# Messages of a graph network by seven products, edges later in the block, and an opening in another order

## The chip, the cores and the metric

The kernel runs on one core of a Trainium2 chip, in f32 throughout. The metric is the device time of one execution in microseconds (us); lower is better. Five engines work beside each other, each with its own queue in order: PE (TensorE, with its weight loads shown as PEld), DVE (VectorE), ACT (ScalarE), POOL (GpSimd) and SP (SyncE, which here only issues DMAs; ACT issues some too). They wait for each other by semaphores.

## The reference

The input x is 128 batches of 128 nodes with 256 features, adj is 128 adjacency matrices of 128x128. Two layers, each x + layer(relu(layernorm(x))). With h the normed input, layer 0 computes for each batch:

```
xc    = h transposed (features x nodes)
conv  = bn2(conv1d(relu(bn1(conv1d(xc, conv1_w))), conv2_w, 17 taps, pad 8))
x_conv= relu(conv + xc) transposed back
s     = h @ w_se.T + b_se                      # 3 numbers for each node
dist  = |s_n|^2 + |s_m|^2 - 2 s_n . s_m
A     = exp(-dist) * adj
msg   = relu(h @ w_msg.T + b_msg)
x_nmp = A @ msg
gi    = concat(x_conv, x_nmp) @ w_ih.T + b_ih  # 512 -> 768: r, z, n
gh    = h @ w_hh.T + b_hh                      # 256 -> 768: r, z, n
r, z  = sigmoid(gi_r + gh_r), sigmoid(gi_z + gh_z)
out   = (1 - z) * tanh(gi_n + r * gh_n) + z * h
```

Layer 1 is five small graph convolutions (256 to 512 to 256 features) over five fixed groups of the first 25 nodes of each batch, weighted by a softmax and added.

## The kernel before

Features lie on the partitions, in C = 2 halves of 128; the 128 batches are 32 blocks of BB = 4 (T = 512 columns). The stages follow each other, named here with their times in the profiled execution:

1. 0 to about 170 us, the heads of the first 64 batches (`heads`, L264; `head_stats`, `head_norm`, `head_turn`, `head_conv1`, `head_spectra`, L184 to L249): layer norm on DVE with a power on POOL (L196), transposes on PE (L212), the 1-wide convolution (L226), and the forward Fourier products (L241). In between, written out by hand through `some_spectra` (L364), the spectra of the 17-tap weights are made on PE (L165) in eight chunks; each loads a tile `w2` (L152, two buffers), issued on ACT's queue when the chunk before has ended (L371), and writes its result to `vd` in memory (L175). `constants()` (L119) folds the first batch norm into the weights `wc1` of L226; it runs up to its first `yield` after the first transposes (L385).
2. About 170 to 280 us and 390 to 489 us, `spectral` (L285) for the first and the second 64 batches: products by frequency (L312, L317), with the weights' spectra `v` read from `vd` (L294, three buffers, on SP's queue) and their sums `vs` made on POOL (L309). Between the two, 280 to 390 us, the heads of the second 64 batches. `gate_weights` (L331) makes sums of the gate weights on POOL inside the second spectral stage.
3. 489 to about 1780 us, `gates` for the 32 blocks (L592). The gates are four units (L602): r from three inputs (h, x_conv, x_nmp), the part of n from h, the part of n from the two others, and z from three. Each unit multiplies in quarters by a scheme of seven products in place of eight (L604 to L633), for which the inputs are first turned into sums `t` by `gate_inputs` (L578: x_nmp on DVE, the others on POOL) and the products are combined on ACT, DVE and POOL while they leave the PSUM banks. `bank()` (L92) hands out the eight banks in rotation.
4. Up to 1917.7 us, the rest of layer 1 (L833), which otherwise is woven into stage 3 with `back` (L750).

Around the change: while the units of block i go on, `step()` (L1006) is called after each product, and on every other turn it advances the generator `beside_gates(i + 1)` (L954), which makes what block i + 1 will need: `messages` (L509, two halves), `conv_out` (L490, two halves), `edge_terms` (L532, transposes of the distance terms `lr`), `edges` (L541, the exponentials) and `x_nmp` (L556, two halves), with the parts of `back(i - 1)`, called `ends`, between. What is left is finished in the hook `nxt` (L1021), in the z unit, which then makes the inputs of block i + 1 with `gate_inputs`. In messages, each of the four batches is one bank with two matmuls of 259 columns (256 of the message, 3 of the distance):

```python
nc.tensor.matmul(ps[:, :D + 3], ht[:, c, b * N:(b + 1) * N], wms[:, c, :], start=c == 0, stop=c == C - 1)
nc.vector.tensor_tensor(msg[:, b, :], ps[:, :D], bms[:, :D], op=ALU.add)
nc.vector.tensor_tensor(lr[:, 1, b, 0:3], ps[:, D:D + 3], bms[:, D:], op=ALU.add)
```

In the first block there is no earlier block to work beside: `begin` (L987) runs up to the edges ahead of it, and `sums_ahead` (L993) finishes it inside the first unit.

Of the kernel before, what the change touches and what calls it, by code (L numbers as in the profile page):

```python
# [13 lines left out]
P = 128  # L14
# [12 lines left out]
HID = 512  # L27

# [46 lines left out]
def gnn_kernel(ctx: ExitStack, tc: tile.TileContext, io, out0: bass.AP, out1: bass.AP):  # L75
# [38 lines left out]
    def constant_loads():  # L114
        nc.sync.dma_start(vec, io["vec"])
        nc.sync.dma_start(wc1, io["wc1"].rearrange("(c p) o -> p c o", p=P))
        nc.sync.dma_start(fd, io["fd"])
# [31 lines left out]
    vd = dram.tile([C, D // WCH, P, LW, WCH], F32, tag="vd", name="vd")  # L149
    yd = [dram.tile([HG, 2, LW, D], F32, tag=f"yd{h}", name=f"yd{h}") for h in range(NH)]  # L150

    def taps_load(pool, c, q, queue, split=1):  # L152
        w2 = pool.tile([P, WCH // 4, P], F32, tag="w2", name="w2", bufs=2)
# [4 lines left out]
    def weight_spectra(pool, c, q, w2):  # L158
# [16 lines left out]
        nc.scalar.dma_start(vd[c, q], sp)  # L175
# [109 lines left out]
    def spectral(bp, X, h, amid):  # L285

        for p0 in range(0, NP_, 4):
            amid.get(p0, lambda: None)()
            ys = bp.tile([P, 4, 2, D], F32, tag="ys", name="ys", bufs=2)
            for p in range(p0, p0 + 4):  # L290
                if p % 2 == 0:
                    v = bp.tile([P, C, D // WCH, 4, WCH], F32, tag="v", name="v", bufs=3)
                    for c in range(C):
                        nc.sync.dma_start(v[:, c], vd[c, :, :, 2 * p:2 * p + 4, :].rearrange("q i d o -> i q d o"))  # L294
# [36 lines left out]
    def gate_weights():  # L331
        tt = nc.gpsimd.tensor_tensor
        for k in range(3):
# [9 lines left out]
    with front as es:  # L343
# [7 lines left out]
        with ExitStack() as ws:  # L351
# [7 lines left out]
            nc.scalar.dma_start(gt, io["gt"])  # L359
            taps = [taps_load(wp, *todo[0], nc.sync, split=4)]  # L360
# [3 lines left out]
            def some_spectra(k=1):  # L364
                for _ in range(k):
                    if not spectra and todo:
                        spectra.append(weight_spectra(wp, *todo.pop(0), taps.pop(0)))
                    if spectra and next(spectra[0], STOP) is STOP:
                        spectra.pop(0)
                        if len(todo) > 1:  # L370
                            taps.append(taps_load(wp, *todo[1], nc.scalar))  # L371
# [7 lines left out]
            nc.sync.dma_start(fw, row("fw", 5))  # L379
            head_stats(hk, 0)  # L380
            some_spectra()
            head_norm(0)
            some_spectra()
            head_turn(hk, 0)
            consts = constants()  # L385
            next(consts)
            some_spectra()
# [13 lines left out]
        wms = gw.tile([P, C, D + 3], F32)  # L401
        bms = gw.tile([P, D + 3], F32)
# [4 lines left out]
        def small_loads():  # L407
            nc.sync.dma_start(idm, io["idm"])
            nc.sync.dma_start(wms, io["wms"].rearrange("(c p) o -> p c o", p=P))
            nc.sync.dma_start(bms, row("bms", D + 3))  # L410
# [79 lines left out]
    def conv_out(i):  # L490
# [4 lines left out]
        for o in range(C):  # L495
# [7 lines left out]
            u = wk.tile([P, T], F32, tag="el", name="u", bufs=2)  # L503
            nc.vector.scalar_tensor_tensor(u, ps, sc2[:, o:o + 1], ht[:, o, :], op0=ALU.mult, op1=ALU.add)  # L504
            nc.scalar.activation(xc[:, o, :], u, AF.Relu, bias=sh2[:, o:o + 1])
# [3 lines left out]
    def messages(i):  # L509

        ht = hts[i]
        msg = wk.tile([P, BB, D], F32, tag="msg", name="msg", bufs=1)
        for b in range(BB):
            ps = bank()
            for c in range(C):
# [652 lines left out]
```

## Time and profile before

| | |
|---|---|
| median of 3 runs | 1919.29 us (1916.35 to 1928.1) |
| profiled execution, its own time | 1919.48 us |
| its span, first to last instruction | 1917.7 us |
| granted TensorE clock, mean | 0.995 |
| busy: PE, PEld, DVE, ACT, POOL | 1890.3, 1646.4, 1303.9, 720.5, 609.1 us |
| stage 3 without its begin, 520 to 1780 us: PE, DVE, ACT, POOL busy | 1258.6, 922.4, 492.1, 435.9 us |
| L516 (messages), PE | 512 records of 128x259 |
| L517 and L518, DVE | 128 of 128x256, mean 414 ns; 128 of 128x3, mean 149 ns |
| DMA | 248872 packets, 265.8 MB |

An f32 matmul leaves two records in the profile. Matmuls overlap in the array, so the busy time of one record (385 ns for L516) is longer than the distance from its start to the next start; what a matmul costs is that distance. The chain of waits lists, in order of time, the piece of work that the end depended on at each moment, its start, its length, and how many instructions it holds. The list of waits gives, for one engine and line, what it waited for, the sum, the number of times and the longest.

### The profile page before, as it was taken

To read this page: it belongs to the slowest core of one execution; us is meant where nothing else is said; L and a number is where in the kernel's file an instruction comes from. 1 tells how busy PE (TensorE), PEld (TensorE's weight loads), DVE (VectorE), ACT (ScalarE), POOL (GpSimd) and SP (SyncE) were. 2 spreads that over 40 slices of the span, in tenths; PEclk is the share of its full clock that TensorE was granted. 3 is DMA by queue.
4 is the path that set the end of the run, shared out by engine and by line. 5 is a ranking of instruction groups with operands and counts; after the bars stand their busy time and mean duration, and the time that the engine had idled before them with its cause. 6 is when DMAs were issued, how large, how long until landed. Compare 5 with 4: busy or idle time off the path is not lost.

```text
span 1917.7 us, 30432 instructions
## 1 busy us (share of the span) xinstructions
PE 1890.3 (99%) x10610; PEld 1646.4 (86%) x10610; DVE 1303.9 (68%) x3247; ACT 720.5 (38%) x1555; POOL 609.1 (32%) x678
## 2 busy tenths in 40 slices
PE   8999999999999999999999999999999999999998
PEld 7888889988788888888888888888888888888887
DVE  5676557744677777777666677777756677787643
ACT  4553114411333343343343443333343434334334
POOL 1012531255234334433322233433322233443300
PEclk9999999999999999999999999999999999999999
DMA  8786896379842333333234433233334434222135
GB/s 322 288 312 226 297 311 235 121 241 306 256 117 73 74 95 76 81 90 106 71 94 97 130 97 87 73 82 108 75 90 97 144 72 107 65 78 71 36 92 151
DMA packets 248872, 265.81 MB, mean 139 GB/s; under 512 B 106866, under 2 KB 223943, under 8 KB 244239
## 3 DMA queue, kind: packets, MB, share of 16 engines
q1 hardware_dynamic: 236639, 196.70, 36.9%
q10 hardware_dynamic: 12080, 67.16, 9.0%
q8 instruction: 85, 1.39, 0.3%
q14 instruction: 68, 0.56, 0.1%
HBM read 178.66 MB, written 85.14 MB: 138 GB/s over the span
## 4 chain that ended last, share of the span: by engine, by line
PE 88%; DMA 4%; DVE 4%; issue 2%; ACT 1%; POOL 1%; SPq 0%; ACTq 0%; POOLq 0%; DVEq 0%
PE bank L612 45%; PE bank L317 6%; PE bank L516 5%; PE bank L937 5%; PE bank L877 5%; PE bank L226 4%; PE bank L312 3%; PE bank L563 3%; PE bank L498 3%; PE bank L241 3%; PE bank L165 2%; PE bank L501 1%; PE bank L788 1%; PE bank L856 1%; DMA v<-vd 1%
## 5 line engine op out<-in xcount | busy, mean ns | idle before, releaser
L612 PE MATMUL bank<-t,sw 128*128 128x256 f32 x1152 | 291.6, 380 | 0.7 <-DVE u L504 0.7
L625 POOL TENSOR_TENSOR u<-u,m 128x256 f32<-128x256 f32 x128 | 93.2, 728 | 612.7 <-ACT m L623 545.0
L612 PEld LDWEIGHTS bank<-t,sw 128*128 128x128 f32 x1152 | 215.8, 191 | 31.1 <-issue 2.3
L612 PE MATMUL bank<-t,wih 128*128 128x256 f32 x768 | 197.2, 379 | 0.0
L612 PEld LDWEIGHTS bank<-t,wih 128*128 128x128 f32 x768 | 143.4, 190 | 19.3 <-issue 0.5
L309 POOL TENSOR_TENSOR vs<-v 128x512 f32<-128x512 f32 x78 | 101.3, 1318 | 114.8 <-DMA v<-vd 49.4
L516 PE MATMUL bank<-wms,ht 128*128 128x259 f32 x512 | 124.1, 385 | 0.0
L226 PE MATMUL bank<-wc,ht 128*128 128x256 f32 x512 | 121.4, 391 | 1.6 <-ACT ht L213 1.6
L612 PE MATMUL bank<-xn,wih 128*128 128x256 f32 x384 | 114.9, 381 | 3.6 <-DVE xn L566 3.6
L612 PE MATMUL bank<-t,whh 128*128 128x256 f32 x384 | 115.0, 381 | 0.0
L612 PE MATMUL bank<-xc,wih 128*128 128x256 f32 x384 | 114.8, 381 | 0.0
L937 PE MATMUL bank<-w,hh 128*125 128x256 f32 (+9 forms) x480 | 113.5, 380 | 1.0 <-DVE hh L882 1.0
L226 PEld LDWEIGHTS bank<-wc,ht 128*128 128x128 f32 x512 | 98.0, 196 | 16.7 <-ACT ht L213 3.5
L516 PEld LDWEIGHTS bank<-wms,ht 128*128 128x128 f32 x512 | 98.3, 192 | 15.1
L612 PE MATMUL bank<-ht,whh 128*128 128x256 f32 x384 | 109.9, 380 | 0.0
L877 PE MATMUL bank<-ax,w 128*128 128x500 f32 (+8 forms) x416 | 107.0, 396 | 0.7 <-DMA w<-in_w_dram 0.7
L520 ACT ACTIVATE msg<-msg 128x512 f32<-128x512 f32 x64 | 40.3, 630 | 174.1 <-DVE msg L517 174.1
L630 DVE TENSOR_TENSOR u<-bank,u 128x256 f32<-128x256 f32 x128 | 53.7, 420 | 73.6 <-PE bank L612 73.5
L196 POOL TENSOR_TENSOR rs<-ve,mhalf 128x4 f32<-128x4 f32 x32 | 32.3, 1009 | 217.8 <-DVE ve L194 217.8
L307 DVE SCALAR_TENSOR_TENSOR s<-X 128x256 f32<-128x256 f32 x78 | 47.3, 612 | 79.4 <-PE bank L317 79.1
L937 PEld LDWEIGHTS bank<-w,hh 128*125 128x125 f32 (+9 forms) x480 | 84.3, 177 | 19.2 <-DVE hh L882 1.4
L657 ACT ACTIVATE nn<-nn,vec 128x512 f32<-128x512 f32 x64 | 46.2, 722 | 133.4 <-DVE nn L656 133.4
(187 smaller groups left out, 4279.5 us busy)
## 6 DMA issues: line engine op xcount, KB each, us to landing
v<-vd SPq DMA_DIRECT2D x80, 512.0 KB
vd<-sp ACTq DMA_DIRECT2D x8, 2560.0 KB
yd<-ys ACTq DMA_DIRECT2D x40, 512.0 KB
w<-in_w_dram SPq DMA_DIRECT2D x40, 512.0 KB
htd<-ht ACTq DMA_DIRECT2D x32, 512.0 KB
ht<-htd SPq DMA_DIRECT2D x32, 512.0 KB
ym<-yd SPq DMA_DIRECT2D x32, 512.0 KB
xt<-in_xT_dram SPq DMA_DIRECT2D x32, 512.0 KB
```

The source lines that it names most:

```text
L226: nc.tensor.matmul(pv[:, bb, :], ht[:, c, b * N:(b + 1) * N], wc1[:, c, :], start=c == 0, stop=c == C - 1)
L241: nc.tensor.matmul(ps[:, bb * 2 * LW:(bb + 1) * 2 * LW], h1[:, 2 * h + bb, c * P:(c + 1) * P], fd, start=True, stop=True)
L309: nc.gpsimd.tensor_tensor(vs, vr, vi, op=ALU.add)
L312: nc.tensor.matmul(p1[:, :D], a[:, c], vs[:, c], start=c == 0, stop=c == C - 1)
L317: nc.tensor.matmul(ps[:, k * D:(k + 1) * D], u[:, c], w[:, c], start=c == 0, stop=c == C - 1)
L498: nc.tensor.matmul(ps[:, b * N:(b + 1) * N], ym[:, b, o * P:(o + 1) * P], idm, start=b == 0, stop=False)
L516: nc.tensor.matmul(ps[:, :D + 3], ht[:, c, b * N:(b + 1) * N], wms[:, c, :], start=c == 0, stop=c == C - 1)
L563: nc.tensor.matmul(ps[:, b * N:(b + 1) * N], msg[:, b, c * P:(c + 1) * P], e[:, b, :], start=True, stop=True)
L612: nc.tensor.matmul(ps, w, d, start=n == 0, stop=n == len(pairs) - 1)
L625: nc.gpsimd.tensor_tensor(got["u4"], got["u2"], got["m5"], op=ALU.add)
L877: nc.tensor.matmul(pv[:, q - q0, :], w1s[k5 + g][:, c, q * P:(q + 1) * P], xv[:, c], start=c == 0, stop=c == C - 1)
L937: nc.tensor.matmul(ps[:n1, :D], hh[:, q, at:at + n1], w2s[k5 + g][:, q, :], start=q == 0, stop=q == HID // P - 1)
```

## The change

The messages are made by the same scheme of seven products as the gates: two batches to a product, 130 columns each (256 + 3 padded to 2 x 130), from the weights' quarters and their sums `swm`, which `gate_weights` makes in an additional step on POOL, and from h and its sums t2. The last product (p4) needs t4 of the block, so `gate_inputs(i, (2,))` is called one block ahead, with two buffers. The results are combined by six additions out of PSUM on DVE, one addition in SBUF on DVE, a copy on ACT and two additions on POOL; the distances come out of the message tile by a copy. `edges` goes two turns later, into the unit of n's inputs, and `x_nmp` follows one turn later than before. `conv_out` works in xc itself without a tile u; in block 0 the second half of xn is copied by ACT. In the opening, `vec` is loaded on ACT's queue ahead of the first x, `constants()` runs up to its first yield ahead of the first norm, three steps of the tap spectra in place of two come ahead of the first transposes, and w2 has three buffers, the third filled early by SP. `vd` is laid out by pairs of frequencies, so that a read takes contiguous 4 KB for each partition, and the write goes in pieces of 1 KB. In numbers of instructions, PE goes from 5500 to 5692, DVE 3249 to 3248, ACT 1648 to 1681, POOL 683 to 752.

```diff
@@ -25,6 +25,7 @@
 HID = 512
+MW = 130
@@ -112,7 +113,6 @@
     def constant_loads():
-        nc.sync.dma_start(vec, io["vec"])
         nc.sync.dma_start(wc1, io["wc1"].rearrange("(c p) o -> p c o", p=P))
@@ -146,11 +146,11 @@
     htd = [dram.tile([P, C, T], F32, tag=f"ht{i}", name=f"htd{i}") for i in range(NBLK)]
-    vd = dram.tile([C, D // WCH, P, LW, WCH], F32, tag="vd", name="vd")
+    vd = dram.tile([C, NP_ // 2, P, D // WCH, 4, WCH], F32, tag="vd", name="vd")
     yd = [dram.tile([HG, 2, LW, D], F32, tag=f"yd{h}", name=f"yd{h}") for h in range(NH)]
...
     def taps_load(pool, c, q, queue, split=1):
-        w2 = pool.tile([P, WCH // 4, P], F32, tag="w2", name="w2", bufs=2)
+        w2 = pool.tile([P, WCH // 4, P], F32, tag="w2", name="w2", bufs=3)
         for t in range(0, WCH // 4, WCH // 4 // split):
@@ -172,7 +172,7 @@
             yield
-        nc.scalar.dma_start(vd[c, q], sp)
+        nc.scalar.dma_start(vd[c, :, :, q].rearrange("u i d o -> i u (d o)"), sp.rearrange("p (u d) o -> p u (d o)", d=4))
@@ -291,7 +291,7 @@
                     for c in range(C):
-                        nc.sync.dma_start(v[:, c], vd[c, :, :, 2 * p:2 * p + 4, :].rearrange("q i d o -> i q d o"))
+                        nc.sync.dma_start(v[:, c], vd[c, p // 2])
                 vr, vi = v[:, :, :, 2 * (p % 2), :], v[:, :, :, 2 * (p % 2) + 1, :]
@@ -330,6 +330,15 @@
         tt = nc.gpsimd.tensor_tensor
+
+        a11, a12, a21, a22 = wms[:, 0, 0], wms[:, 1, 0], wms[:, 0, 1], wms[:, 1, 1]
+        s2, s3, s4 = (swm[:, j] for j in range(3))
+        tt(s3, a11, a21, op=ALU.subtract)
+        tt(a21, a21, a22, op=ALU.add)
+        tt(s2, a21, a11, op=ALU.subtract)
+        tt(s4, a12, s2, op=ALU.subtract)
+        tt(bms[:, 1], bms[:, 1], bms[:, 0], op=ALU.subtract)
+        yield
         for k in range(3):
@@ -357,6 +366,7 @@
             nc.scalar.dma_start(gt, io["gt"])
+            nc.scalar.dma_start(vec, io["vec"])
             taps = [taps_load(wp, *todo[0], nc.sync, split=4)]
@@ -367,8 +377,8 @@
                         spectra.pop(0)
-                        if len(todo) > 1:
-                            taps.append(taps_load(wp, *todo[1], nc.scalar))
+                        if len(todo) > 2:
+                            taps.append(taps_load(wp, *todo[2], nc.scalar))
                         some_spectra()
@@ -377,14 +387,15 @@
             nc.sync.dma_start(fw, row("fw", 5))
+            taps.append(taps_load(wp, *todo[2], nc.sync))
             head_stats(hk, 0)
+            consts = constants()
+            next(consts)
             some_spectra()
...
             some_spectra()
+            some_spectra()
             head_turn(hk, 0)
-            consts = constants()
-            next(consts)
-            some_spectra()
             head_stats(hk, 1)
@@ -398,16 +409,17 @@
         idm = gw.tile([P, N], F32)
-        wms = gw.tile([P, C, D + 3], F32)
-        bms = gw.tile([P, D + 3], F32)
+        wms = gw.tile([P, C, 2, MW], F32)
+        bms = gw.tile([P, 2, MW], F32)
+        swm = gw.tile([P, 3, MW], F32)
         wih = gw.tile([P, 2 * C, 3 * D], F32)
...
             nc.sync.dma_start(idm, io["idm"])
-            nc.sync.dma_start(wms, io["wms"].rearrange("(c p) o -> p c o", p=P))
-            nc.sync.dma_start(bms, row("bms", D + 3))
+            nc.sync.dma_start(wms, io["wms"].rearrange("(c p) (q o) -> p c q o", p=P, q=2))
+            nc.sync.dma_start(bms.rearrange("p q o -> p (q o)"), row("bms", 2 * MW))
@@ -500,29 +512,52 @@
                              start=False, stop=True)
-            u = wk.tile([P, T], F32, tag="el", name="u", bufs=2)
-            nc.vector.scalar_tensor_tensor(u, ps, sc2[:, o:o + 1], ht[:, o, :], op0=ALU.mult, op1=ALU.add)
-            nc.scalar.activation(xc[:, o, :], u, AF.Relu, bias=sh2[:, o:o + 1])
+            nc.vector.scalar_tensor_tensor(xc[:, o, :], ps, sc2[:, o:o + 1], ht[:, o, :], op0=ALU.mult, op1=ALU.add)
+            nc.scalar.activation(xc[:, o, :], xc[:, o, :], AF.Relu, bias=sh2[:, o:o + 1])
             yield
...
-        ht = hts[i]
-        msg = wk.tile([P, BB, D], F32, tag="msg", name="msg", bufs=1)
-        for b in range(BB):
-            ps = bank()
-            for c in range(C):
-                nc.tensor.matmul(ps[:, :D + 3], ht[:, c, b * N:(b + 1) * N], wms[:, c, :], start=c == 0, stop=c == C - 1)
-            nc.vector.tensor_tensor(msg[:, b, :], ps[:, :D], bms[:, :D], op=ALU.add)
-            nc.vector.tensor_tensor(lr[:, 1, b, 0:3], ps[:, D:D + 3], bms[:, D:], op=ALU.add)
-            if b % 2:
-                nc.scalar.activation(msg[:, b - 1:b + 1, :], msg[:, b - 1:b + 1, :], AF.Relu)
-                if b == 1:
-                    yield
-        msgs[i] = msg
+
+        msg = wk.tile([P, BB, 2, MW], F32, tag="msg", name="msg", bufs=1)
+        b11, b12, b21, b22 = quarters(hts[i])
+        t1, t2, t3, t4 = (ts[i][2][:, m] for m in range(4))
+        s2, s3, s4 = (swm[:, m] for m in range(3))
+        ops = ((wms[:, 0, 0], b11), (wms[:, 1, 0], b21), (s4, b22), (wms[:, 1, 1], t4), (wms[:, 0, 1], t1), (s2, t2), (s3, t3))
+
+        def product(j):
+            w, d = ops[j - 1]
+            ps = bank()[:, :2 * MW].rearrange("p (b o) -> p b o", b=2)
+            for b in range(2):
+                nc.tensor.matmul(ps[:, b, :], d[:, b * N:(b + 1) * N], w, start=True, stop=True)
+            return ps
+
+        def part(name):
+            return wk.tile([P, 2, MW], F32, tag=name, name=name, bufs=2)
+
+        def biases(q):
+            return bms[:, q, None, :].to_broadcast([P, 2, MW])
+
+        m1, u2, m5, u4, u3 = (part(n) for n in ("m1", "u2", "m5", "u4", "u3"))
+        nc.vector.tensor_tensor(m1, product(1), biases(0), op=ALU.add)
+        nc.vector.tensor_tensor(msg[:, 0:2, 0], product(2), m1, op=ALU.add)
+        nc.vector.tensor_tensor(u2, product(6), m1, op=ALU.add)
+        nc.scalar.copy(m5, product(5))
+        nc.gpsimd.tensor_tensor(u4, u2, m5, op=ALU.add)
+        nc.gpsimd.tensor_tensor(u2, u2, biases(1), op=ALU.add)
+        yield
+        nc.vector.tensor_tensor(msg[:, 2:4, 0], product(3), u4, op=ALU.add)
+        nc.vector.tensor_tensor(u3, product(7), u2, op=ALU.add)
+        nc.vector.tensor_tensor(msg[:, 0:2, 1], u3, product(4), op=ALU.subtract)
+        nc.vector.tensor_tensor(msg[:, 2:4, 1], u3, m5, op=ALU.add)
+        mf = msg.rearrange("p b q o -> p b (q o)")
+        for b in range(0, BB, 2):
+            nc.scalar.activation(mf[:, b:b + 2, :D], mf[:, b:b + 2, :D], AF.Relu)
+        msgs[i] = mf
         sv = lr[:, 1, :, 0:3]
-        nc.vector.tensor_scalar(lr[:, 0, :, 0:3], sv, 2.0, None, op0=ALU.mult)
+        nc.vector.tensor_copy(sv, mf[:, :, D:D + 3])
+        nc.vector.tensor_scalar(lr[:, 0, :, 0:3], mf[:, :, D:D + 3], 2.0, None, op0=ALU.mult)
         s2 = wk.tile([P, BB, 3], F32, tag="sse", name="sse", bufs=2)
@@ -562,7 +597,7 @@
                                  start=True, stop=True)
-            if c:
+            if c and i:
                 nc.vector.tensor_copy(xn[:, c, :], ps)
@@ -581,7 +616,7 @@
             d = d[i]
-            t = wk.tile([P, 4, H], F32, tag=f"t{k}", name=f"t{k}")
+            t = wk.tile([P, 4, H], F32, tag=f"t{k}", name=f"t{k}", bufs=1 + k // 2)
             b11, b12, b21, b22 = quarters(d)
@@ -970,9 +1005,11 @@
                 yield
+            next(ends, None)
+            yield
+            yield
+
             edges(i)
-            yield
-            next(ends, None)
             yield
@@ -984,10 +1021,12 @@
     degs = degrees(*degree_loads())
+    gate_inputs(0, (2,))
     begin = beside_gates(0)
...
         next(begin)
-    gate_inputs(0, (2, 0))
+    gate_inputs(0, (0,))
+    gate_inputs(1, (2,))
     held = [6]
@@ -1022,7 +1061,9 @@
             if i + 1 < NBLK:
-                gate_inputs(i + 1)
+                gate_inputs(i + 1, (0, 1))
+            if i + 2 < NBLK:
+                gate_inputs(i + 2, (2,))
@@ -1103,8 +1144,9 @@
     d.update(_spectral_constants())
-    d["wms"] = cc(np.concatenate([w["w_msg"], w["w_se"]]).T)
-    d["bms"] = cc(np.concatenate([w["b_msg"], w["b_se"]]))
+    pad = np.zeros((2 * MW - w["w_msg"].shape[0] - 3, w["w_msg"].shape[1]), np.float32)
+    d["wms"] = cc(np.concatenate([w["w_msg"], w["w_se"], pad]).T)
+    d["bms"] = cc(np.concatenate([w["b_msg"], w["b_se"], pad[:, 0]]))
     d["wih"] = cc(w["w_ih"].T)
```

## The prediction

> **What bounds the kernel now.** I read the page first, then the spans of the core, the critical chain inside one block of the steady stretch, the waits of PE, the chain over the first 30 us and the groups of instructions.
>
> ```profile
> span 1917.7 us, 30432 instructions
> PE 1890.3 (99%) x10610; PEld 1646.4 (86%) x10610; DVE 1303.9 (68%) x3247; ACT 720.5 (38%) x1555; POOL 609.1 (32%) x678
> ```
>
> PE is the bound from end to end. A busy share of 99% says little by itself, so I asked the chain for one block, 875 to 915 us:
>
> ```profile
> 874.94 4.32 PE bank L612 x20
> 879.26 1.75 PE bank L516 x8
> 881.01 2.59 PE bank L612 x12
> 883.60 1.75 PE bank L516 x8
> ...
> 900.58 0.89 PE bank L563 x8
> 901.48 1.73 PE bank L612 x8
> ```
>
> There is no foreign piece in it: PE issues matmul records back to back, and a block lasts 36.92 us from one L516 to the next. An f32 matmul leaves two records, so 8 message matmuls are 16 records. The spacing follows: 259 columns 1.75/8 = 218 ns, 256 columns (L612) 216 ns, 128 columns (L563) 0.89/8 = 112 ns. Start-to-start differences of the single records give 136 ns for 160 columns (L241) and again 112 ns for 91 and for 48 columns: below about 130 columns something else than the moving columns sets the pace. Only work taken from PE, or waits of PE, can change the time. The waits that the profile names:
>
> ```profile
> PE bank L165 <- DMA gt<-in_gt_dram: 3.9, 1, 3.9
> PE bank L612 <- DVE xn L566: 3.6, 1, 3.6
> PE bank L212 <- issue: 2.6, 1, 2.6
> PE bank L165 <- DMA w<-in_w2t_dram: 2.4, 1, 2.4
> PE bank L241 <- ACT X L249: 2.3, 1, 2.3
> ```
>
> All are singles, in the opening and at the change to the gates (489 to 520 us); the steady blocks have none.
>
> **What the Trainium skill says.** "TensorE: Matmul & The Clock Gate", section Back-to-back issue gap: the spacing is set by weight load and matmul together; section LDWEIGHTS: a load costs its columns over 1.2, about 107 ns for 128, whatever the rows. The trace agrees: 48, 91 and 128 columns all at 112 ns, with 128-column loads. "SBUF — State Buffer", Who interferes with whom: GpSimd shares a port with VectorE's second operand. The trace agrees: the Pool subtraction L588 takes 907 and 1172 ns at 877.7 and 879.4 us, where the same shape alone takes 720. "ScalarE: Activation LUTs", What ACT_TABLE_LOAD costs: about 1283 ns, which is the trace's duration too.
>
> **The change part by part.**
>
> *Messages, PE.* Removed per block: 16 records of 259 columns x 218.5 ns = 3.50 us. Added: seven products of two batches, 14 matmuls, 28 records of 130 columns. No row shows 130. The floor is 112 ns; the line through 160 (136) and 256 (216) gives 136 - 30 x 0.83 = 111, so the bounds are 112 and 116 (a little overhead on the two extra columns). I take 112: 28 x 0.112 = 3.14 us. Gain 0.36 us, x 32 blocks = 11.5; at 116 it is 8. Multiplying less by one eighth gives only a tenth, because short products fall on the weight floor.
>
> *Messages, evictions.* Out: four DVE additions of 128x256 (414 ns) and four of 128x3 (149): 2.25 us. In: six PSUM additions of 128x260 at about 420, one SBUF addition 410, a small copy 150: 3.1 us on DVE; a copy on ACT (0.36); two additions on Pool (0.73 to 1.17 each); ACT's two Relus stay. None is on the path if banks come free in time. Eight banks rotate in order of issue, so the ninth product after p1 (order 1,2,6,5, two products of the gates, 3,7,4) is p4, and it waits for p1's eviction. From the block shown: messages start at 879.10 by single records, p4 is due at 884.37; DVE does its first message eviction at 883.35 (it is still at the state update of the block before), so p1's is done at 883.77: margin about 0.6 us. The next, a gates product that needs p2's bank, has 1.4 us. Pool's last t of this block's input (L589) ends at 882.9 against 884.37. Cost 0, margin thin.
>
> *Edges.* They move two turns later, x_nmp one. From edges to x_nmp's second half: a table load 1.28, four exps, a DVE product, together about 3.3 us against 3.9 of products between. Cost 0, margin 0.6. The transposes of the distances at 891.3 need the lr chain, done about 888.7. Cost 0. Three small lines of DVE go, one copy comes.
>
> *t2 a block ahead.* Pool's order stays t0 then t2, merely for another block; two buffers. 0. The u tile goes (xc in place): 0.
>
> *gate_weights.* Five Pool operations of 128x130 (about 0.4 each, 2 us) in the second spectral stage, where Pool is busy 56.5 of 99 us: 0.
>
> *Third tap buffer.* Before, at 56.2 us the chain turns to the DMA of w2 and PE stands 2.4 to 2.6 us at 67. With the load issued one chunk earlier it has landed. -2.6, between -2.6 and 0: the DMA engines are 75 to 90% busy until 140 us, so a third early load also delays others.
>
> *vd layout.* Reads become 4 KB per packet in place of 1 KB. Packet records: 1 KB 50 ns, 4 KB 160 ns; a v load of 512 KB pays 32 x 50 = 1.6 us per engine before, 8 x 160 = 1.3 after. Stage times at 81 to 87% DMA share thus fall under the load's limit. The stalls that spacing shows at 230 to 252 (L309 on Pool waits 49.4 us for v, mostly covered) and at 467 are together about 3.3; I take -2.5 (-3.3 to -1). The write becomes 1 KB pieces in place of 20 KB: 2.5 MB over 16 engines are 160 x 8 = 1280 packets x 50 ns = 64 us of engine time against 53 (64 x 834 ns). The last write is issued at 139.3 and the first v load follows it; it lands some 1 to 2 us later, and PE's stall of 2.5 us at 153 grows: +1.0 (-0.5 to +2).
>
> *Opening.* The constants' chain goes ahead of the first norm:
>
> ```profile
> 7.74 2.51 issue
> 10.25 2.25 PE bank L212 x8
> 12.50 3.65 PE bank L165 x64
> 16.14 2.00 PE bank L138 x8
> 18.15 1.94 PE bank L165 x32
> 20.09 5.26 PE bank L226 x16
> ```
>
> Nine small DVE operations, two Pool pows (0.7 to 1.0 each, with a hand-over both ways) and a 512-wide copy are about 3.7 us before head_norm(0), so the transposes go from 10.25 to about 14; one more spectra step (32 records, 1.8 us) is pulled into the gap of 2.5 us, which grows. L226, the first thing that depends on both, starts at about 21.5 instead of 20.1. +1.5 (+0.5 to +2.5). vec on ACT's queue, ahead of ln0, delays ln0 by its own issue (an issue on ACT's queue lasts 0.33 to 0.35 in the chain); taken into that range.
>
> *Change to the gates, 489 to 520.* The stall of 3.6 us on xn is set by the chain degrees, edges, x_nmp. i=0's xn copy goes to ACT, behind which DVE's reductions no longer stand; but the DVE list puts the degree reductions, gated by loads landing at 507 to 512, ahead of the first state update, and the first p6 must wait for Pool's t2, some 1.8 us. 0 (-4 to +2). Block 1's stalls at 557 and 560 (0.8 and 1.0): -0.5.
>
> *Sum* on the profiled execution's own 1919.48: -11.4 - 2.6 - 2.5 + 1.0 + 1.5 + 0 - 0.5 = -14.5, so 1905. The median of the runs, 1919.29, is the same to 0.2. The runs spread from 1916.35 to 1928.1; about 1% (19.2 us) is what a measurement of this kernel can tell from no change.
>
> **The rivals.**
>
> *A: as summed*, 1905, own range 1900 to 1911.
>
> *B: PE gains less in the messages.* Spacing 116 to 120, or a wait of 0.2 us in each p4, takes 4 to 7 back: 1909 to 1916, say 1912. For it: no row of 130 columns, and the margin of 0.6. Against: the line through the neighbours ends on the floor.
>
> *C: the early stalls go as well.* The opening costs nothing (1.5), the xn stall (3.6) halves, 557 and 560 and the 1.3 at 38 vanish: 1905 - 1.5 - 2 - 2.5 = 1899, and up to 1896. For it: xn's copy leaves DVE, which was the releaser. Against: the degree loads land when they did.
>
> *D: slower, by DVE's queue.* DVE's fourth message addition needs u4 from Pool, which needs the ACT copy of p5. DVE is in order: behind the addition stand the evictions of the gates' products, and behind these PE's banks. Pool has subtractions of 1.17 us back to back until 882.9. If u4 comes late, DVE stands and PE with it. A delay under 0.6 us is free, each further one counts in full: over 1% slower needs 33.5 us beyond 1905, 1.1 us in each of 31 blocks, so an eviction 1.7 us late. Place: between the second half of the messages and L501; price then about 1942. For it: Pool goes up by two operations in its busiest spot, DVE by 0.85 us. Against: Pool finishes 1.5 us before p4 is due, and DVE has 127 us idle in 442 of the steady stretch (314.7 busy).
>
> *E: the change does nothing visible there*: PE would have to be bound elsewhere. The steady chain has no such piece, so it is contained in B.
>
> **How the numbers follow.** A 0.53, B 0.21, C 0.17, D 0.09. The predicted time is A's, 1905. The range holds A and B and most of C: 1897 to 1916; D and the edge of C are left out. Faster by over 1% (under 1900.1): most of C, a sliver of A: 0.17. Slower by over 1% (over 1938.5): most of D, 0.07. Within 1%: 0.76.
>
> **What would show it.** Messages' row: 28 x 32 = 896 records of 128x130 with 112 ns spacing, a piece of eight lasting 0.89 to 0.90 us; period 36.56 in place of 36.92. No wait of PE on a message addition in the steady blocks; if there is one, D or B. No w2 wait near 67. L226's first start near 21.5. The stall before the first gates still 2 to 4 us. A block period of 36.9 or more makes the prediction wrong in its main term; a period right and a total off by over 5 us makes the opening or the change of stage wrong.

## The result, and the profile after

The changed kernel takes 1943.28 us (median of 4 runs, 1934.57 to 1944.25) against 1918.37 (4 runs); the ratio is 1.0111, 95% interval 1.0077 to 1.0145. It is slower, and outside the forecast's range. The first lines of the page after:

```profile
span 1942.0 us, 31350 instructions
PE 1892.0 (97%) x10994; PEld 1654.5 (85%) x10994; DVE 1320.2 (68%) x3246; ACT 722.3 (37%) x1588; POOL 666.0 (34%) x747
```

PE's busy time is nearly the same as before, though the messages now take less of it, and the span is 24.3 us longer: the time went into gaps, and, as shown below, into matmuls at a lower clock. Where, the moments of the traces tell (us from the span's start; read off the start of the named instruction):

| | before | after | difference |
|---|---|---|---|
| first layer norm (x has landed) | 6.08 | 11.23 | +5.2 |
| first transposes | 10.25 | 18.86 | +8.6 |
| first convolution | 20.02 | 26.77 | +6.8 |
| first spectral product | 173.14 | 197.36 | +24.2 |
| first spectral product, second half | 385.61 | 411.87 | +26.3 |
| transposes of distances, fifth block | 633.22 | 658.23 | +25.0 |
| the same, last block | 1766.64 | 1790.03 | +23.4 |
| end | 1917.69 | 1941.99 | +24.3 |

Nearly all of the loss is there at the first spectral product. Over the 27 blocks that follow the fifth's transposes only 1.6 us come back, where 9.7 were forecast. The waits of PE (sum, times, longest):

```profile
PE bank L165 <- ACT sp L173: 10.2, 5, 3.7
PE bank L212 <- DVE ln L202: 8.4, 1, 8.4
PE bank L165 <- DMA gt<-in_gt_dram: 3.9, 1, 3.9
PE bank L226 <- ACT ht L213: 3.5, 5, 1.1
```

The wait for w2 is gone, as forecast. The first row was one wait of 0.4 us before: PE waits for ACT to copy tap spectra out of PSUM. The chain of the first 200 us shows what ACT did instead:

```profile
1.68 9.53 DMA ln<-in_x_dram
...
18.86 2.10 PE bank L212 x8
...
43.38 0.45 ACTq L175
43.92 5.25 ACTq L155
49.21 0.43 ACT sp L173
49.69 1.99 PE bank L165 x26
51.68 6.56 PE bank L226 x16
...
68.50 3.30 ACTq L155
...
88.94 4.39 ACTq L155
...
103.89 3.67 PE bank L226 x16
...
108.78 3.39 ACTq L155
...
164.50 3.39 ACTq L214
```

ACTq is ACT's queue at a DMA issue. Right after six of the eight writes of vd (L175) the next issue, a tap load (L155) or once a store (L214), holds ACT for 3.3 to 5.3 us; before, the tap loads took 0.37 to 2.00, and this was the longest:

```profile
37.02 2.00 ACTq L155 DMA_DIRECT2D w<-in_w2t_dram  x1
```

Behind a held issue stand the copies (L173) and behind these PE. The same 16 records of L226 take 6.56 us right after such a gap and 3.67 later: the granted clock falls too. By windows (length, busy times of PE, PEld, DVE, ACT and POOL, clock, DMA share, GB/s), after and then before:

```profile
44.00:58.00 14.00, 9.98 (x55) 8.04 (x53) 4.28 (x15) 3.58 (x11) 1.01 (x1) 0.63 0.87 321
```

```profile
44.00:58.00 14.00, 14.00 (x185) 12.22 (x183) 9.41 (x27) 7.96 (x21) 1.96 (x2) 1.00 0.63 226
```

Over the first 170 us the mean clock is 0.91 against 0.97. So the 24.2 us are roughly 13.6 of waits (10.2 for ACT, 5.8 more at the transposes, 2.4 less for w2) and an estimated 10 of a slower clock (0.06 x 170).

The messages themselves did what was forecast. One block of the chain after, 900 to 940 us:

```profile
903.16 1.79 PE bank L533 x16
904.95 2.59 PE bank L647 x12
907.54 1.34 PE bank L533 x12
...
918.87 0.90 PE bank L823 x4
```

28 records of 130 columns in 3.13 us are 112 ns each. But the product L823 takes 0.90, where the same product took 0.72 before (there L788), and a plain block, one without layer 1's steps between its gates, lasts 36.70, not 36.55:

```profile
896.84 0.72 PE bank L788 x4
```

### The profile page after: what moved, and what is told of

It is laid out like the page before. It is cut to its first block, busy times and chain, and to the rows that moved or that the text cites. A ratio compares the mean times of both kernels' runs of the same rounds, so it can differ in the third digit from the quotient of the medians.

```text
span 1942.0 us, 31350 instructions
## 1 busy us (share of the span) xinstructions
PE 1892.0 (97%) x10994; PEld 1654.5 (85%) x10994; DVE 1320.2 (68%) x3246; ACT 722.3 (37%) x1588; POOL 666.0 (34%) x747
## 4 chain that ended last, share of the span: by engine, by line
PE 87%; DVE 5%; DMA 4%; ACTq 1%; ACT 1%; issue 1%; POOL 1%; SPq 0%; DVEq 0%; POOLq 0%
PE bank L647 43%; PE bank L317 7%; PE bank L972 5%; PE bank L533 5%; PE bank L912 5%; PE bank L226 4%; PE bank L312 3%; PE bank L598 3%; PE bank L510 3%; PE bank L241 2%; DMA nt<-in_adjN_dram 1%; PE bank L165 1%; PE bank L823 1%; PE bank L513 1%; PE bank L891 1%
## 5 line engine op out<-in xcount | busy, mean ns | idle before, releaser
L226 PE MATMUL bank<-wc,ht 128*128 128x256 f32 x512 | 122.3, 393 | 3.6 <-ACT ht L213 3.5
L226 PEld LDWEIGHTS bank<-wc,ht 128*128 128x128 f32 x512 | 98.2, 197 | 19.7 <-ACT ht L213 6.4
L307 DVE SCALAR_TENSOR_TENSOR s<-X 128x256 f32<-128x256 f32 x78 | 53.0, 683 | 79.8 <-PE bank L317 79.5
L972 PEld LDWEIGHTS bank<-w,hh 128*125 128x125 f32 (+9 forms) x480 | 83.9, 178 | 23.4 <-DVE hh L917 4.3
L314 ACT COPY k<-bank 128x256 f32<-128x256 f32 x78 | 29.0, 373 | 171.3 <-DVE ys L318 59.7
L912 PEld LDWEIGHTS bank<-ax,w 128*128 128x128 f32 x416 | 69.9, 190 | 19.3 <-issue 12.3
L317 PE MATMUL bank<-v,s 128*128 128x256 f32 x312 | 80.4, 380 | 2.7 <-issue 2.5
```

The source lines that it names most:

```text
L226: nc.tensor.matmul(pv[:, bb, :], ht[:, c, b * N:(b + 1) * N], wc1[:, c, :], start=c == 0, stop=c == C - 1)
L317: nc.tensor.matmul(ps[:, k * D:(k + 1) * D], u[:, c], w[:, c], start=c == 0, stop=c == C - 1)
L912: nc.tensor.matmul(pv[:, q - q0, :], w1s[k5 + g][:, c, q * P:(q + 1) * P], xv[:, c], start=c == 0, stop=c == C - 1)
L972: nc.tensor.matmul(ps[:n1, :D], hh[:, q, at:at + n1], w2s[k5 + g][:, q, :], start=q == 0, stop=q == HID // P - 1)
```

## Experiments

Twelve kernels, each run beside the kernel before, whose own median moved between 1916.62 and 1920.58 us from one occasion to the next. Ratios are to it, with 95% intervals. Moments are read as in the table above: first convolution, first spectral product.

**Old layout of vd.** The changed kernel with

```diff
-    vd = dram.tile([C, NP_ // 2, P, D // WCH, 4, WCH], F32, tag="vd", name="vd")
+    vd = dram.tile([C, D // WCH, P, LW, WCH], F32, tag="vd", name="vd")
-        nc.scalar.dma_start(vd[c, :, :, q].rearrange(...), sp.rearrange(...))
+        nc.scalar.dma_start(vd[c, q], sp)
...
```

and the read of v back to its old form with it.

> The changed kernel with the old layout of vd alone (writes in 20 KB pieces, reads in 1 KB pieces). In the changed kernel the next tap load and the next htd store stand on ACT's queue behind the write of vd and take 5.25, 3.30, 4.39, 3.39 and 3.39 us to issue, where before the longest such issue took 2.00. Theory 1, the many small pieces of the write fill ACT's queue and hold ACT at its next issue: those five fall to 0.3 to 2 us, the first spectral product comes 12 to 17 us earlier than the 197.4 us of the changed kernel, total about 1928. Theory 2, the write itself is slower on the DMA engines and holds back the tiles: the same gain here. Rival, the opening order alone made the loss: nothing, 1943.

Measured: 1921.86 us, 1.0006 (0.9987 to 1.0026). First spectral product at 169.22, 28 us earlier than in the changed kernel. Of these, 3.1 are there already at the first convolution (23.70), where the layout has no part; from there to the first spectral product it is 145.52 us against 170.59, so the small pieces cost 25.1. That is more than expected, and the clock stays up as well (mean 1.00 over the first 170 us, 0.91 in the changed kernel). So the layout's write made almost the whole loss; both theories 1 and 2 say this.

**The same small pieces, written by SP.**

```diff
-        nc.scalar.dma_start(vd[c, :, :, q].rearrange(...), sp.rearrange(...))
+        nc.sync.dma_start(vd[c, :, :, q].rearrange(...), sp.rearrange(...))
```

> The changed kernel with the new layout of vd, its write issued on SP's queue instead of ACT's. Theory 1 (ACT held at its next issue behind the write): as good as the old layout, the first spectral product 12 to 17 us earlier than 197.4, total about 1928, because SP's own next issues are loads made well ahead. Theory 2 (the 1 KB pieces are too slow on the DMA engines): no gain, 1940 to 1946, PE still waits for ACT's copies to sp, 10 us in all.

Measured: 1916.72 us, 0.998 (0.9969 to 0.9992), 11 us under what theory 1 expected; first spectral product at 167.00. The pieces are the same, only their queue differs, as the row of ACT's DMA queue in the page shows (packets, MB, share of 16 engines), in the changed kernel and here:

```profile
q10 hardware_dynamic: 31536, 66.14, 9.1%
```

```profile
q10 hardware_dynamic: 10928, 45.16, 6.2%
```

And ACT's issues of tap loads, in order of time, here; the longest two of five:

```profile
41.32 1.50 ACTq L155 DMA_DIRECT2D w<-in_w2t_dram  x1
...
71.60 1.75 ACTq L155 DMA_DIRECT2D w<-in_w2t_dram  x1
```

Theory 2, that the pieces are too slow on the DMA engines, falls. Theory 1 stands: what costs is that ACT's next DMA issue is held, and with it ACT's copies, while its queue holds a write of many pieces.

Two more readings support it. The hold moves with the write and comes with the pieces. Two of the kernels below are the kernel before with the write on SP's queue; they differ only in the layout. SP's next issue after the same write, with small pieces and then with pieces of 20 KB:

```profile
35.33 0.37 SPq L175 DMA_DIRECT2D vd<-sp  x1
35.79 7.27 SPq L182 DMA_DIRECT2D ln<-in_x_dram  x1
```

```profile
36.02 0.34 SPq L175 DMA_DIRECT2D vd<-sp  x1
36.45 0.39 SPq L182 DMA_DIRECT2D ln<-in_x_dram  x1
```

No copy stands behind SP, and in these two executions the small pieces cost 2.4 us from the first convolution to the first spectral product (144.52 and 142.15), not 25.1. And the hold ends when enough pieces have gone: by the records of packets in the changed kernel, 1014 to 1459 pieces had passed on ACT's queue since the write's issue when a held issue ended (a write has 2560), and the two issues that came only after 2664 and 2676 pieces took 0.33 us. What limit of the queue this is, the traces don't show.

**Old opening order.** vec back on SP's queue, `constants()` behind `head_turn`, one step of spectra moved behind it; the write of vd still on ACT.

```diff
+            some_spectra()
+            head_norm(0)
+            some_spectra()
+            head_turn(hk, 0)
             consts = constants()
             next(consts)
             some_spectra()
-            head_norm(0)
-            some_spectra()
-            some_spectra()
-            head_turn(hk, 0)
```

> The changed kernel with the old opening order (vec on SP's queue, constants after the first transposes, two steps of spectra ahead of them); third tap buffer and new layout of vd kept. Theory: the constants' chain and the late first x cost 8.6 us at the first transposes and 6.7 at the first convolution, so these come at 10 to 12 us and 20 to 21 us, and the total falls by about 7, to 1936. Rival, the third tap load delays the first x: the first layer norm still starts near 11 us and nothing is gained. Rival, the waits behind the writes of vd swallow the gain: first convolution early, first spectral product still near 197.

Measured: 1937.31 us, 1.0086 (1.0058 to 1.0115); first layer norm at 6.17, first convolution at 20.11, first spectral product at 190.27. Six to seven us, as expected; the third tap load does not delay x.

**The messages alone.** The changed kernel with the old vd, the old opening and two tap buffers.

> The changed kernel without its three early parts (old layout of vd, old opening order, two tap buffers): the messages by seven products, the inputs a block ahead, the later edges. By the forecast's sum 11.5 us under before, 1907. By the trace of the changed kernel, where a block lasts 36.70 instead of 36.92 and the blocks with layer 1 give 1.8 us back twice, 2 to 6 us under before: 1913 to 1917, and the first spectral product at 173 as before.

Measured: 1921.42 us, 1.0009 (0.9994 to 1.0024). Both expectations missed: nothing is gained. By block, the trace gains 0.22 in each plain one and loses 3.9 in blocks 12 to 16 (219.85 us against 215.93, from the transposes of distances in one to those in the other) and 1.5 in 22 to 26. These are the blocks with layer 1's steps between the gates. There, in the kernel with the write on SP (219.97), the profile of PE in order of time:

```profile
1074.68 0.69 PE L972 MATMUL bank<-w,hh 128*120 128x256 f32 x2 [1.55 <-ACT hh L919]
1076.25 0.83 PE L972 MATMUL bank<-w,hh 128*120 128x256 f32 x2 [0.87 <-DVE hh L917]
1076.88 1.06 PE L647 MATMUL bank<-t,whh 128*128 128x256 f32 x2
1077.73 1.91 PE L647 MATMUL bank<-t,wih 128*128 128x256 f32 x4
```

PE waits for hh, the hidden features of layer 1, which DVE and ACT take out of PSUM, and then runs at a lower clock (four records in 1.91 us; 1.03 in the same view at 1066). DVE is late because of nt, a small adjacency block that comes by DMA: in the chain there, two loads of nt last 5.58 and 3.11 us, and hh follows on them. DVE's waits for DMAs (ae is the adjacency that the parts of `back` work on; hn, which comes up below, is the normed input of their last product, L823), before, and then in the kernel with the write on SP:

```profile
DVE nt L815 <- DMA nt<-in_adjN_dram: 16.4, 21, 2.0
...
DVE ae L768 <- DMA ae<-in_adjE_dram: 2.7, 4, 1.2
```

```profile
DVE nt L850 <- DMA nt<-in_adjN_dram: 56.0, 30, 4.8
DVE ae L803 <- DMA ae<-in_adjE_dram: 37.0, 26, 2.7
```

And SP's queue in one plain block, before and then with the write on SP. The load of ae stood ahead of the five stores of xa, now it stands behind them:

```profile
823.74 0.30 SPq L743 DMA_DIRECT2D ae<-in_adjE_dram  x1
825.92 0.40 SPq L453 DMA_DIRECT2D at<-in_adjT_dram  x1
826.43 3.19 SPq L798 DMA_DIRECT2D xa<-ab  x5
```

```profile
813.54 3.18 SPq L833 DMA_DIRECT2D xa<-ab  x5
816.76 0.60 SPq L469 DMA_DIRECT2D yr<-yd  x1
817.47 0.30 SPq L778 DMA_DIRECT2D ae<-in_adjE_dram  x1
```

Theory 3: the later edges moved the fourth part of `back`, whose stores these are, and added a turn, by which layer 1 slips. The sum of the waits alone doesn't set the loss: in the changed kernel DVE waits 56.4 us for nt and 37.1 for ae, and blocks 12 to 16 take only 217.20.

**Edges at their old turns**, seven products kept, write of vd on SP.

```diff
-            next(ends, None)
-            yield
-            yield
-
             edges(i)
             yield
+            next(ends, None)
+            yield
             yield
```

> The kernel with the write of vd on SP's queue (1916.7 us, profiled 1917.1), and in it the edges and the fourth part of the block before back at their old turns; the seven products stay. In that kernel DVE waits 56.0 us for nt (30 times) and 37.0 us for ae (26 times), before 16.4 and 2.7; its blocks 12 to 16 take 219.97 us against 215.93 before. Theory 3, the turn of edges shifts layer 1 by a step in each block and its loads behind other issues on SP's queue: the waits fall to about 16 and 3, blocks 12 to 16 last 214.5, a plain block 36.56, and the total falls by 8 to 11, to 1906 to 1909. Rival, the seven products' larger load on DVE makes DVE late for layer 1, and nothing changes: 1914 to 1919. Rival, the old turn lets PE wait for the transposed distances or for the edges in every block: a plain block over 36.8, slower than 1917.

Measured: 1907.56 us, 0.9944 (0.9929 to 0.996). Blocks 12 to 16 take 214.99, and the waits are

```profile
DVE nt L850 <- DMA nt<-in_adjN_dram: 22.7, 23, 2.6
...
DVE ae L803 <- DMA ae<-in_adjE_dram: 3.0, 4, 1.3
```

Theory 3 holds on the side of layer 1: the old order takes the loss there away, though the run puts back the fourth part and the turn together. The plain block misses: 36.84, not 36.56, because at the old turn PE waits 0.17 us for a bank in each (DVE's addition there waits for Pool, Pool for ACT's copy, which stands behind a Relu) and loses 0.10 more while it restarts.

**vec on SP's queue**, constants ahead of the first norm, write of vd on SP.

```diff
-            nc.scalar.dma_start(vec, io["vec"])
     def constant_loads():
+        nc.sync.dma_start(vec, io["vec"])
```

> The kernel with the write of vd on SP's queue, and vec loaded by SP behind the first taps as before; the constants' chain stays ahead of the first norm. Where vec stands ahead of x on ACT's queue, the first layer norm started at 8.2, 9.0 and 11.2 us, where it did not at 6.1 to 6.3. If vec in that place delays x: start at about 6.2, first transposes at 12.5 to 14 instead of 16.6, first convolution 2 to 3 us earlier, at about 22. If vec now comes too late for the constants' chain (its packets ended at 7.05 before): the transposes stay near 16. Total 1913 to 1916.

Measured: 1911.64 us, 0.9963 (0.9949 to 0.9978). First layer norm at 6.34, transposes 13.97, first convolution 21.89; the total is a little under the expected. So the chain of constants costs 1.9 us at the convolution, and vec ahead of x on ACT's queue another 1.8 to 4.9 (first convolution at 23.70 with the old vd, 24.55 in the two kernels with the write on SP, 26.77 in the changed kernel). In the records of packets, x's 512 pieces pass from 3.60 to 5.64 us before and from 4.40 to 10.69 after; why they trail is open. Some of it is spread: with the opening of the kernel before, one execution below has its first layer norm at 7.25, the others at 6.1 to 6.3; with vec ahead of x the four are at 8.2 to 11.2.

**All mended**: write on SP, old opening, edges at their old turns; seven products, three tap buffers and the new layout kept.

> What the runs point to as the best: the seven products, the new layout of vd written by SP, three tap buffers, the old opening order with vec on SP's queue, the edges at their old turns. First convolution at 20.2, first spectral product at 163 to 166, a plain block 36.56. Theory 3: 1901 to 1906. If theory 3 falls: 1911 to 1914.

Measured: 1903.51 us, 0.9924 (0.9909 to 0.9939), first spectral product at 162.59. As expected of theory 3, except for the plain block, 36.84 again.

**The kernel before with the new vd, written by SP**, and **the kernel before with the old vd, written by SP**. The second one's edit is

```diff
-        nc.scalar.dma_start(vd[c, q], sp)
+        nc.sync.dma_start(vd[c, q], sp)
```

> The kernel before with the new layout of vd alone, written by SP. By the forecast: reads in 4 KB pieces take 1 to 3.3 us from the spectral stages, the write adds -0.5 to 2: total 1916 to 1920. By the runs with the write on SP (first spectral product 2.2 us earlier than with the old layout though the first convolution was 0.9 later; 3.7 us more in the stage to the second heads): 3 to 6 us under before, 1914 to 1917. If ACT's queue was free of trouble in the kernel before, nothing at the first spectral product: 173.

> The kernel before with its old layout of vd, and only the queue of the write changed, from ACT's to SP's. With the new layout as well, the first spectral product came 8.6 us earlier and the first gates 9.7. If it was the queue: the same here, 163 to 166 and 1908 to 1911. If it was the layout, that is the 4 KB reads: little here, 172 to 174, 1916 to 1919. Forecast of the reads: 1 to 3.3 us between the first spectral product and the gates.

Measured: 1908.42 us, 0.9946 (0.9929 to 0.9963), first spectral product at 164.57; and 1907.72 us, 0.9954 (0.9934 to 0.9974), at 163.35 (173.14 before). So the queue gives all of it, in the kernel before too, and without the hold: there ACT's issues stay as they were (the longest 2.03). The gain goes with PE's waits for w2 and for X, 2.4 and 2.3, which are gone, and with a clock of 0.99 in place of 0.97 over the first 170 us (an estimated 3.4 us). The wait for w2 the records of packets explain: before, the tap load issued at 56.21 starts to move at 63.63, when the write ahead of it on ACT's queue is nearly through, and ends at 69.46; with the write on SP, the same load, issued at 56.29, moves from 59.13 to 64.27. How the wait for X goes was not taken apart. From the first spectral product to that of the second half it is 212.39 us with the 4 KB reads, 212.89 without, and the second spectral stage takes 102.64 us in both: the reads in 4 KB give 0.5.

**Edges one turn later, x_nmp at its old turn, the fourth part ahead of them.**

```diff
             next(ends, None)
             yield
-            yield
-
             edges(i)
```

> The best kernel so far (1903.5 us, blocks of 36.83) with the edges one turn later instead of at their old turn, the fourth part of the block before ahead of them, and x_nmp still at its old turn, so that the number of turns in a block is the old one. At the old turn PE waits 0.17 us in each block for a gates product's bank (ACT has the distances' Relu and the table load in front) and restarts slowly, 0.27 in all; two turns later a block is 36.70, but layer 1 slips. If the extra turn makes layer 1 slip: blocks 12 to 16 stay at 214 to 215, nt waits near 20 us, and blocks fall to 36.55 to 36.7: 1896 to 1901. If the place of the fourth part or of the edges does it: blocks 12 to 16 near 219, ae and nt waits of 37 and 56 us, 1905 to 1911.

Measured: 1912.87 us, 0.9971 (0.996 to 0.9981), above both expectations. It is slower than the one with the edges at their old turns, but it goes some way to part two causes:

```profile
DVE ae L803 <- DMA ae<-in_adjE_dram: 71.2, 25, 4.8
DVE nt L850 <- DMA nt<-in_adjN_dram: 24.9, 18, 3.7
```

With the old number of turns nt's waits and blocks 12 to 16 (215.63) are nearly back; with the fourth part ahead, ae stays late. The plain block is 36.92 to 36.97, because edges and x_nmp are now too near (PE waits 0.14 for e, with 0.10 of restart), and because the product L823 waits for hn as in the changed kernel (0.05, with 0.10).

**Loads ahead**: later edges as in the change, write on SP, old opening; ae with two buffers, nt and dck loaded six packs ahead instead of five.

```diff
-        ae = l1.tile([P, GW], F32, tag="ae", name="ae", bufs=1)
+        ae = l1.tile([P, GW], F32, tag="ae", name="ae", bufs=2)
-        if 0 <= j + 5 < NPK:
+        if 0 <= j + 6 < NPK:
...
```

> The later edges as in the changed kernel (two turns later, one more turn in a block), with the write of vd by SP and the old opening order, and the loads that had become late made earlier: ae with two buffers, nt and dck one pack further ahead (9 and 4 buffers; lt and xl give up their second one for the room). In the changed kernel's order on SP, the five xa stores stand ahead of ae's load, which they did not before, and DVE waits 37 us for ae and 56 for nt. If late loads are what the later edges cost: ae's wait under 5 us, nt's under 35, a plain block 36.55 to 36.60 instead of 36.70, blocks 12 to 16 at 214 to 217 instead of 219.97; total 1898 to 1905. If the slip of layer 1 costs by itself, whatever the loads: blocks 12 to 16 at 219 again, 1907 to 1911.

Measured: 1905.56 us, 0.994 (0.992 to 0.9961). Half a miss: blocks 12 to 16 take 216.8, though 22 to 26 still lose 2.4 against before, and the second buffer does nothing for ae (44.2 us of waits), as its load keeps its place in SP's order, and the plain block stays at 36.70.

**The fourth part one turn later**, behind ae's load again, with the later edges, and nt six packs ahead as in the run above; ae with one buffer.

```diff
-            next(ends, None)
             yield
+            next(ends, None)
             yield
-
             edges(i)
```

> As the run with the loads ahead (later edges, write of vd by SP, old opening order, nt one pack ahead), but ae with one buffer again, and the fourth part of the block before one turn later, two turns after its third part as before and behind ae's load in SP's order. There DVE still waited 44 us for ae with two buffers, and PE lost 0.05 and a slow restart of 0.10 in each block at the product that needs hn. If the place of the fourth part makes both: ae's wait under 5 us, no wait for hn, a plain block 36.55; blocks 12 to 16 near 216.5 as there, total 1900 to 1903. If ae and hn are late for another cause: blocks of 36.70, 1904 to 1908.

Measured: 1897.12 us, 0.9898 (0.9863 to 0.9933), the fastest of all and 3 us under its expectation; somewhat under half of its gain is that of the write's queue alone (0.9954, above). Its page and two of its waits:

```profile
PE 1867.8 (99%) x10994; PEld 1642.6 (87%) x10994; DVE 1344.9 (71%) x3246; ACT 722.5 (38%) x1588; POOL 645.4 (34%) x747
```

```profile
DVE nt L850 <- DMA nt<-in_adjN_dram: 43.1, 25, 4.7
DVE ae L803 <- DMA ae<-in_adjE_dram: 8.6, 11, 2.1
```

ae's wait stays over the 5 us that were expected. A plain block lasts 36.55, as this run's expectation has it (36.56 in the prediction), and in its chain the product that needs hn is back at 0.72:

```profile
841.04 0.72 PE bank L823 x4
```

Blocks 12 to 16 take 214.66, with the later edges and the additional turn. So the turn by itself need not cost; whether it would without the earlier loads of nt is not shown. DVE still waits 43 us for nt, while PE's waits for hh are down to 0.2: that wait seems to cost only where hh stands behind it. Which of the two edits freed hh was not taken apart.

## Why the prediction was wrong, point by point

*The step that failed* is the one on the layout of vd: "it lands some 1 to 2 us later, and PE's stall of 2.5 us at 153 grows: +1.0 (-0.5 to +2)". It priced the write by the time of its pieces on the DMA engines, 64 us against 53, and looked for who waits for the data. That stall did not grow: PE's wait for X, 2.3 us before, is 1.6. The engine that issues waits: ACT's next issue took 3.3 to 5.3 us in place of at most 2.0, with copies behind it that free PE's banks. Measured, in place of 1.0: 25.1 us from the first convolution to the first spectral product against the old layout on the same queue (170.59 and 145.52), and 28.1 against the same layout on SP's queue (142.45). On SP's queue the term comes out near its size, at 2.4 us. Rival D's text asks what stands behind a waiting DVE; that was not asked of an issue on ACT. That the total, 1943, comes near rival D's price of 1942 is chance.

In the profiled executions the forecast is 38.8 us off (14.5 under before, measured 24.3 over). Of these, 5.3 lie ahead of the first convolution (6.8 against 1.5), 19.1 from there to the first spectral product (17.5 over, where the sum had 1.6 under; the write's cost less what the third tap buffer gave back), and 8.1 in the 27 blocks from the fifth on (1.6 us won, where the sum had 9.7). The rest is spread over the spectral stages, the first blocks and the end.

*The reads in 4 KB*, -2.5 (-3.3 to -1): measured -0.5, outside its range. The step counted stalls at 230 to 252 and at 467 as the reads' to save; what did hold PE there was not taken apart.

*The opening*, +1.5 (+0.5 to +2.5): the constants' chain cost 1.9, well inside. The term for vec was mis-sized: it was put at one issue of 0.33 to 0.35, and with vec ahead of x the first convolution comes a further 1.8 to 4.9 us later.

*Third tap buffer*, -2.6: the wait is gone; between the all-mended kernel and the one before with the new vd on SP, otherwise alike up to there, 2.0 at the first spectral product. With the old layout and the write on ACT it may be worth more: from the first convolution to the first spectral product 152.40 us in the messages-alone kernel with two buffers, 145.52 with three, but there the openings differ too.

*Messages on PE*, -0.36 a block: 3.13 us against 3.50, right, and the 36.55 of the last run shows that all of it can be had. *Evictions*, cost 0: right. Only one wait on a message addition appears (0.5 us, once), and rival D, DVE's queue holding PE in the messages, didn't happen. The slower side came from another place than any rival had. The forecast's own sign for its main term, a period of 36.56, was met in part (36.70). Its other sign, a total off by over 5 us with the period right, named the opening and the change to the gates; of the miss only 5.3 us lie ahead of the first convolution, and the change to the gates stayed inside its range.

*Edges*, "Cost 0, margin 0.6": failed as a step, though the margin itself held. The working counted what edges and x_nmp need. It did not count what moves with them: the fourth part of `back` with five stores on SP's queue, and a turn more for `beside_gates`. Cost: 0.14 in each plain block (the product waits for hn and restarts), and layer 1. The two stretches of blocks 12 to 16 and 22 to 26 take 3.9 and 1.5 us more than before in the kernel with the messages alone and 1.3 more each in the changed kernel, where four plain blocks would have won 1.5. In the kernels with the write on ACT in small pieces the first of them loses 1.3 to 1.6, in the four others with the edges and the loads of the change 3.6 to 4.4; why is open. By the run with the messages alone all this ate the whole gain of the messages, 1921.42 against 1920.58.

*Change to the gates*, 0 (-4 to +2): from the first spectral product of the second half to the fifth block's transposes the difference goes from 26.3 to 25.0, inside, though this stretch also holds a spectral stage and four blocks.

*A reading*: the transposes of the distances, put at 891.3, start at 891.69 in the trace, which only widens the margin given.

## What to carry to other kernels

A DMA's price has two sides: the time of its pieces, and the next issue on the same queue. Before a write is cut into small pieces, look at what the issuing engine has to do behind it; if that frees PSUM banks, try the write from an engine that computes nothing. In this kernel that was worth 10.9 us (1918.63 to 1907.72) even with the large pieces. And where a step written out by hand moves a turn, list every DMA that moves with it and what it is moved past: here the place of one part, with five stores on SP's queue, made 8.4 us between the last two runs, against 11.5 forecast for the change on PE.

## What the runs showed of the hardware

A wait of PE can cost more than its length. After three waits of 3.66, 2.64 and 2.73 us in the changed kernel (up to 49.69, 72.37 and 112.75) the granted clock was 0.50 over the next 4 us, and 0.61 as the mean of 1077 to 1081 us in the kernel with the write on SP, after two waits of 1.55 and 0.87. But after waits of 1.65 and 2.24 us (up to 179.75 and 523.23 in the changed kernel) it was 1.00, so the length of a wait alone doesn't decide. Where it was looked at, a wait of only 0.04 to 0.17 us was followed by about 0.10 more until the spacing was back to its usual value, for L823, for x_nmp and for the gates alike.

The Trainium skill has the first in "TensorE: Matmul & The Clock Gate", section What's actually happening: half the clock after an idle window of about 3.4 us. The traces agree on the half (a spacing of 0.427 us in place of 0.216 after the two waits), but here a single wait of 2.64 us was enough, and so were the two with 2.4 us in all within 3.1.
